# Attention of a two-layer graph network: two visits of eight heads in place of four visits of four

## The chip, the cores and the metric

The kernel runs on one core of one Trainium2 chip. The metric is device time in microseconds (us). Engines are named as in the profile: PE (TensorE matmuls), PEld (its weight loads), DVE (VectorE), ACT (ScalarE), POOL (GpSimd), SP (SyncE, which issues the DMAs here). All data are float32.

## The reference, cut to what matters

64 graphs of 256 nodes with 512 features pass two layers. Layer 0 is masked attention with eight heads of width 64, layer 1 a graph attention with one score per node.

```python
# layer 0
h = maximum(layernorm(x), 0)
q, k, v = h @ Wq + bq, h @ Wk + bk, h @ Wv + bv          # 8 heads of 64
attn = softmax(q @ k.T / 8 + (1 - adj) * -1e9)            # per head, 256 x 256
x = x + (attn @ v) @ Wo + bo
# layer 1
h = maximum(layernorm(x), 0); g = h @ W
e = leaky_relu(g @ a1 [:, None] + g @ a2 [None, :]) * adj
x = x + elu(softmax(e) @ g + beta * g)
```

## The kernel before, in words

**Work and order.** Graphs are taken in pairs, p = 0 to 31; pair p holds graphs g0 = 2p and g1 = 2p + 1. The order of every instruction on PE, DVE, ACT and POOL is the order in which the Python code issues it (a manual schedule), so what stands first in the code stands first in its engine's queue. A round of the steady part is `first_half(p)` and then `second_half(p)`; each round works on four pairs at once: q, k and v of pair p+1, attention of graphs around pair p, the output projection (`UnitO`) and layer norm of pair p-1, and layer 1 (`UnitW`) of pair p-2. `start`, `first`, `last` and `end` are the same work at the two ends.

**Units.** Every weight product of a pair is done as seven smaller products (a fast two-by-two block scheme). `Unit.p(i)` (L274) issues product i: four PE instructions of 128x256, which the trace shows as eight, since a float32 matmul is two passes. `products(u, 2, 7, 5)` (L635) issues several, with DVE's and ACT's additions behind them: product 6 has an addition at L285, product 7 one at L288, product 5 is followed by `put2`, product 3 by `put12`, product 2 by `put11`. Products 1 and 2 add up in one PSUM bank, 5 and 3 in another.

**Attention visits.** `scores(b, q)` (L413) computes the scores of four of a graph's eight heads (q is 0 or 1): 8 PE instructions with 64 rows each, two heads side by side in the array. ACT takes the exponential of each head into a `pt` tile (L424), POOL multiplies it by the mask (L425) and adds its two halves into `pp` (L427) for the row sums. `values(b, q)` (L442) multiplies the four `pt` tiles with v (L438, tiles of 32 columns, four heads side by side), sums the `pp` tiles with a matmul against ones (L447), and DVE takes the reciprocal (L449), adds the sums to a range check `acc` (L450) and scales the result into `oT` (L452). `acc` also takes the reciprocals, on POOL (L453), as a function that the next `scores` calls after its second head. A visit is `values` of one group of four heads and `scores` of a later one, back to back on PE; a round has four visits.

**PSUM.** There are eight banks under one tag. A visit takes one for the products with v, one for the sums and four for the scores; a unit takes five.

**Layer 1 scores.** After the output projection, `y_stats_0` to `y_stats_2` (L658 to L666, instructions at L248), `y_scales` (bn_aggr on DVE, then three small POOL instructions, L258 to L260) and `y_normal` (ACT, L507) give the normalised rows `h2` of pair p-1. `y_sums` (L513) is one DVE instruction per node tile and column: `pr = h2 * war` with a running sum into `s12`; a graph needs four. `gat_scores` (L516) transposes these sums with two PE instructions (`pe`, L171) and forms the scores `e` on DVE (L523 twice, L525); `gat_exp` is on ACT (L530); `gat_divide` is three DVE instructions per graph (L535, L537 twice), reading `e` and the constant `betai`; `gat_t` transposes `e` with four PE instructions (`at`, L546); `gat_z` (L559) multiplies it with `h2`.

**Where these stood.** In `second_half`, `y_sums` of graph g1-2 stood behind product 6 of the first q/k unit, `gat_scores` of both graphs of the pair in the second q/k unit, `divide` behind its product 7, and `gat_t` at the start of the v unit.

**Buffers.** `BUFS` gives buffers by tag: 4 for `pt`, 4 for `pp`, 8 for `y`, and separate tags for x (`xt`) and `h2`.

Of the kernel before, what the change touches and what calls it, by code (L numbers as in the profile page):

```python
# [16 lines left out]
P = 128  # L17
# [6 lines left out]
def kernel(ctx: ExitStack, tc: tile.TileContext, x, adj, wq, bq, wk, bk, wv, bv, wo, bo, w, a, beta, out):  # L24
# [33 lines left out]
    BUFS = {"set": 13, "qk": 8, "v": 4, "pt": 4, "xt": 4, "y": 8, "h2": 4, "e": 2, "eT": 2, "m": 2, "c": 3, "u": 4}  # L58
# [17 lines left out]
    def load(p, *which):  # L76
        for g in [2 * p + gi for gi in which or (0, 1)]:
            for t in range(NT):
                XT[g, t] = sb([P, D], "xt", f"x_{g}_{t}", BUFS["xt"])
                nc.sync.dma_start(XT[g, t], x[g, t * P:(t + 1) * P, :])  # L80
# [213 lines left out]
    def combine_31(s, a21, a22, tag="set"):  # L294

        s["tag"] = tag
        s[7] = blk(tag, f"s3_{s['name']}")
        a21(s[7], ALU.subtract, s[1])
        s[5] = blk(tag, f"s1_{s['name']}")
        a22(s[5], ALU.add, s["a21"])  # L300
# [112 lines left out]
    def scores(b, q, between=None):  # L413
        pss = [bank(f"sc_{b}_{q}_{i}") for i in range(4)]
        for pair in range(2):
            qk = QK.pop((b, 2 * q + pair))
            for k in range(NT):
                for h in range(2):
                    hs = slice(h * HD, (h + 1) * HD)
                    nc.tensor.matmul(pss[2 * pair + h][:, k * N:(k + 1) * N], qk[hs, 1, k * P:(k + 1) * P],  # L420
                                     qk[hs, 0, :], start=True, stop=True)
        for i in range(4):
            pt = PT[b, q, i] = blk("pt", f"pt_{b}_{q}_{i}")
            nc.scalar.activation(pt, two(pss[i]), AF.Exp, scale=QSCALE)  # L424
            nc.gpsimd.tensor_tensor(pt, pt, maskT, ALU.mult)  # L425
            pp = PP[b, q, i] = sb([P, N], "pp", f"pp_{b}_{q}_{i}", 4)
            nc.gpsimd.tensor_tensor(pp, pt[:, 0, :], pt[:, 1, :], ALU.add)  # L427
            if between and i in between:
                between[i]()
# [12 lines left out]
    def values(b, q):  # L442

        ps = weigh(V.pop((b, q)), [PT.pop((b, q, i)) for i in range(4)], f"{b}_{q}")
        sums = bank(f"sm_{b}_{q}")
        for i in range(4):
            nc.tensor.matmul(sums[i * HH:(i + 1) * HH, :N], ones[:, :HH], PP.pop((b, q, i)), start=True, stop=True)  # L447
        rec = sb([P, N], "rec", f"rec_{b}_{q}")
        nc.vector.reciprocal(rec, sums[:, :N])  # L449
        nc.vector.tensor_tensor(acc, sums[:, :N], acc, ALU.add)  # L450
        OT[b, q] = blk("set", f"oT_{b}_{q}")
        nc.vector.tensor_tensor(OT[b, q], two(ps), rec.unsqueeze(1).to_broadcast([P, 2, N]), ALU.mult)  # L452
        return lambda: nc.gpsimd.tensor_tensor(acc, acc, rec, ALU.add)  # L453
# [48 lines left out]
    def normal(g, rstd, nmr, tag="h2"):  # L502
        h2 = H2[g] = [sb([P, D], tag, f"h2_{g}_{t}", BUFS[tag]) for t in range(NT)]
        SC[g] = sb([P, NT, 2], "s12", f"s12_{g}", 3)
        for t in range(NT):
            for f in range(2):
                nc.scalar.activation(h2[t][:, f * N:(f + 1) * N], Y[g, f][:, t, :], AF.Relu, bias=nmr[:, t:t + 1],  # L507
                                     scale=rstd[:, t:t + 1])
# [68 lines left out]
    class UnitW(Unit):  # L577

        def __init__(self, p, tags=("m", "c")):
            self.pair, self.o, self.tags = p, {}, tags  # L580
            super().__init__(f"w_{p}", nodes_mm(A.pop(("z", p)), WW))

        def elu(self, gi, fh, src, o=None, step=None):
            g = 2 * self.pair + gi
            if not step:
                m = blk(self.tags[0] if (gi, fh) != (0, 0) else "m", f"m_{g}_{fh}")
                nc.scalar.activation(m, src, AF.Relu, scale=-1.0)
                nc.scalar.activation(m, m, AF.Exp, scale=-1.0)  # L588
                self.o[gi, fh] = (o or blk(self.tags[1], f"o_{g}_{fh}"), m)
            if step is not False:  # L590
                nc.vector.scalar_tensor_tensor(self.o[gi, fh][0], src, 0.0, Y.pop((g, fh)), op0=ALU.max, op1=ALU.add)

        def finish(self, gi, fh, eng):
            g = 2 * self.pair + gi
            o, m = self.o[gi, fh]
# [10 lines left out]
        def put2_sums(self):  # L606
            self.c = blk(self.tags[1], f"o_{2 * self.pair + 1}_1")
# [77 lines left out]
    def residuals(p, tag="y"):  # L685
        for gi, fh in ((0, 0), (1, 1), (1, 0), (0, 1)):
# [27 lines left out]
    def start():  # L714
# [42 lines left out]
        scores(0, 0)  # L757
        shift(0)
        products(uv, 4, 6)
        shift(1)  # L760
        products(uv, 2, 7, 5)
        shift(2)
        products(uv, 3)
        return wo_blocks

    def first():
        add = values(0, 0)
        scores(0, 1, {1: add})
        x_t(1)
        load(2)  # L770
        s = A["h", 1]
        ua, ub, uv = UnitQK(1, 0), UnitQK(1, 1), UnitV(1)
        ua.p(1)
        combine_24(s)
        products(ua, 4, 6)
        prods = project_a()
        prods(0)
        products(ua, 2, 7)
        add = values(0, 1)
        scores(1, 0, {1: add})  # L780
        residuals(0)
        products(ua, 5)
        ub.p(1)
        prods(1)
        products(ub, 4)
        products(ua, 3)
        products(ub, 6)
        prods(2)
        products(ub, 2)
        add = values(1, 0)  # L790
        scores(1, 1, {1: add})
        products(ub, 7, 5)
        uv.p(1)
        products(ub, 3)
        prods(3)
        prods(4)
        products(uv, 4)
        for i in range(2 * NT):
            x_stats(2, i)
        add = values(1, 1)  # L800
        x_scales(2)
        scores(2, 0, {1: add})
        o_blocks(0)
        products(uv, 6, 2)
        x_normals(2, *range(2 * NT))
        products(uv, 7, 5)
        prods(5)
        products(uv, 3)
        combine_24(A["o", 0])
        uo = UnitO(0)  # L810
        uo.p(1)
        uo.p(4)
        add = values(2, 0)
        scores(2, 1, {1: add})
        products(uo, 6, 2)
        return uo


    def first_half(p):
        g0, g1 = 2 * p, 2 * p + 1  # L820
        uw = UnitW(p - 2)
        uw.p(1)
        x_stats(p + 1, 0)
        x_stats(p + 1, 1)
        uw.p(4)
        x_stats(p + 1, 2)
        x_stats(p + 1, 3)
        products(uw, 6, 2, 7, 5)
# [3 lines left out]
        add = values(g0, 0)  # L832
        scores(g0, 1, {1: add})
# [3 lines left out]
        uo = UnitO(p - 1)  # L837
        uo.p(1)
# [8 lines left out]
        products(uo, 2)  # L847
        return uo

    def second_half(p, uo):  # L850
        g0, g1 = 2 * p, 2 * p + 1
        products(uo, 7)
        y_stats_0(p - 1)
        products(uo, 5)
        x_t(p + 1)
        if p + 2 < NP:
            load(p + 2)
        products(uo, 3)
        combine_2(A["h", p + 1])
        add = values(g0, 1)  # L860
        y_stats_1(p - 1)
        y_stats_2(p - 1)
        combine_4(A["h", p + 1])
        scores(g1, 0, {1: lambda: (add(), y_scales(p - 1))})
        ua, ub = UnitQK(p + 1, 0), UnitQK(p + 1, 1)
        products(ua, 1, 4)
        y_normal(p - 1, 1)
        products(ua, 6)
        y_sums(p - 1, 1, 0, 1)
        products(ua, 2)  # L870
        y_normal(p - 1, 0)
        products(ua, 7, 5)
        y_sums(p - 1, 0, 0)
        add = values(g1, 0)
        scores(g1, 1, {1: add})
        products(ua, 3)
        y_sums(p - 1, 0, 1)
        products(ub, 1, 4, 6)
        gat_scores(g1 - 2)
        products(ub, 2)  # L880
        gat_exp(g1 - 2)
        gat_scores(g0 - 2)
        gat_exp(g0 - 2)
        products(ub, 7)
        divide(p - 1)
        products(ub, 5)
        add = values(g1, 1)
        scores(g1 + 1, 0, {1: add})
        if p == NP - 2:
            o_blocks(p, "xt")  # L890
        residuals(p)
        uv = UnitV(p + 1)
        uv.p(1)
        gat_t(g1 - 2)
        gat_t(g0 - 2)
        products(ub, 3)
        products(uv, 4, 6, 2, 7, 5)
        if p == NP - 2:
            return uv
        gat_z(p - 1)  # L900
        products(uv, 3)
        combine_24(A["z", p - 1])

    def last(uv):
        p = NP - 1
        g0, g1 = 2 * p, 2 * p + 1
        combine_24(A["o", p - 1])
        add = values(g0, 0)
        scores(g0, 1, {1: add})
        products(uv, 3)  # L910
# [3 lines left out]
        add = values(g0, 1)  # L914
        scores(g1, 0, {1: add})
        products(uo, 5)
        y_stats_1(p - 1)
        gat_z(p - 2)
# [3 lines left out]
        combine_24(A["z", p - 2])  # L922
        add = values(g1, 0)
        scores(g1, 1, {0: lambda: y_normal(p - 1, 1), 1: add})
        uw = UnitW(p - 2, ("pt", "xt"))
        products(uw, 1, 4)
        y_sums(p - 1, 1, 0, 1)
        products(uw, 6)
        y_normal(p - 1, 0)
        products(uw, 2, 7)  # L930
        uw.finish(0, 0, nc.gpsimd)
        residual(p, 0, 0, "qk")
# [4 lines left out]
        add = values(g1, 1)  # L937
        o_blocks(p)
        residual(p, 1, 1, "qk")
        residual(p, 1, 0, "qk")  # L940
        residual(p, 0, 1, "qk")
        add()
        uw.put2_elu(False)
        uw.p(3)
        uo = UnitO(p)
        uo.p(1)
        uo.p(4)
        y_sums(p - 1, 0, 0)
        combine_24(A["o", p])
        y_sums(p - 1, 0, 1)  # L950
        return uw, uo

    def end(uw, uo):
        p = NP - 1
        g0, g1 = 2 * p, 2 * p + 1
        products(uo, 2)
        gat_scores(g0 - 2)
        gat_exp(g0 - 2)
        uo.p(6)
# [13 lines left out]
        normal(g1, rstd, minus(mr, f"y{g1}"), "qk")  # L973
# [6 lines left out]
        normal(g0, rstd, minus(mr, f"y{g0}"), "qk")  # L980
# [6 lines left out]
        uw = UnitW(p - 1, ("pt", "xt"))  # L987
# [16 lines left out]
        uw.put2_elu()  # L1004
        uw.p(3)
        gat_t(g0)
        uw.put12()
# [9 lines left out]
        uw = UnitW(p, ("pt", "xt"))  # L1017
# [16 lines left out]
    with tc.manual_schedule(engines={ENG.PE, ENG.DVE, ENG.Activation, ENG.Pool}):  # L1034
        WO = start()
        WW = {}
        uo = first()
        second_half(1, uo)
        for p in range(2, NP - 1):
            uv = second_half(p, first_half(p))  # L1040
        end(*last(uv))
# [16 lines left out]
    def general(src, dst, W, mask):  # L1058
        xt = sb([P, NT, D], "x", "fx", 1)
# [145 lines left out]
```

## Time and profile before

| what | value |
|---|---|
| median of 3 runs | 2856.28 us (2855.66 to 2856.35) |
| the profiled execution | 2857.51 us, span 2855.7 us |
| granted PE clock, mean | 0.997 |
| a round of the steady part (one `second_half` to the next in the timeline) | 88.09 us |
| recip L449 | 128 instructions, 1745 ns each |
| DVE `acc<-sm,acc` L450 | 128, 359 ns each |
| POOL `acc<-acc,rec` L453 | 128, 852 ns each |
| DVE `pr<-h,war` L513 | 256, 1228 ns each |
| POOL mask L425 / half sums L427 | 512 each, 1404 / 845 ns |

The span is from the first to the last instruction; the time of an execution has some 2 us more around it. In a timeline, a line is a group of like instructions that follow each other, with the start, the time, the engine, the line of the code and the tiles. PE's matmuls are pipelined and their ends modelled, so that the distance from one start to the next tells more than the time shown.

### The profile page before, as it was taken

The page shows a single profiled execution, that of the slowest core. Times are in us where ns is not written, and L with a number is a line of the kernel's source. Part 1 is how long each engine was busy: PE and PEld are TensorE (multiplying, and loading weights), DVE is VectorE, ACT ScalarE, POOL GpSimd, SP SyncE. Part 2 cuts the span into 40 slices and gives each one's busy share as a digit, 9 for nine tenths or more (in the row PEclk, how much of TensorE's full clock was granted, in tenths as well). Part 3 has the DMA queues.
Part 4 walks back from the last instruction along what each step waited for, and adds up shares of the span by engine and source line. Part 5 has one row for each costly group of instructions (what it writes and reads, how often), then busy time and mean ns, then how long its engine had stood idle before and what let it go on. Part 6 is the DMA issues. An engine that isn't in the chain of part 4 may idle for free. (4 is left out here: it accounts for less than half of the span.)

```text
span 2855.7 us, 46364 instructions
## 1 busy us (share of the span) xinstructions
PE 2837.8 (99%) x18110; PEld 2331.3 (82%) x18110; DVE 2067.1 (72%) x3651; ACT 1045.4 (37%) x2116; POOL 1624.5 (57%) x1592
## 2 busy tenths in 40 slices
PE   9999999999999999999999999999999999999997
PEld 8888888888888888888888888888888888888876
DVE  6776786767867677767777676786767877677767
ACT  3333433333433334333333333343333433334333
POOL 3755655556555556555575555655556655556572
PEclk9999999999999999999999999999999999999998
DMA  5000111100111001110011110111100111001001
GB/s 155 23 31 22 38 45 45 45 15 32 45 45 45 19 27 45 45 45 28 18 45 45 45 33 20 38 45 45 45 16 30 45 45 45 21 25 45 30 20 42
DMA packets 96479, 110.00 MB, mean 39 GB/s; under 512 B 8576, under 2 KB 79488, under 8 KB 96256
## 3 DMA queue, kind: packets, MB, share of 16 engines
q1 hardware_dynamic: 96256, 106.99, 12.0%
q8 instruction: 145, 2.38, 0.4%
q14 instruction: 78, 0.64, 0.1%
HBM read 73.41 MB, written 33.55 MB: 37 GB/s over the span
## 5 line engine op out<-in xcount | busy, mean ns | idle before, releaser
L425 POOL TENSOR_TENSOR pt<-pt,maskT 128x512 f32<-128x512 f32 x512 | 719.0, 1404 | 552.8 <-ACT pt L424 552.8
L427 POOL TENSOR_TENSOR pp<-pt 128x256 f32<-128x256 f32 x512 | 432.9, 845 | 40.2
L424 ACT ACTIVATE pt<-sc 128x512 f32<-128x512 f32 x512 | 264.4, 603 | 338.2 <-PE sc L420 332.0
L513 DVE SCALAR_TENSOR_TENSOR pr<-h,war 128x512 f32<-128x512 f32 x256 | 303.4, 1228 | 57.0 <-ACT h L507 57.0
L596 POOL TENSOR_TENSOR o<-o,m 128x512 f32<-128x512 f32 x40 | 50.6, 1268 | 515.1 <-ACT m L588 463.4
L420 PE MATMUL sc<-qk 64*128 64x256 f32 x2048 | 255.7, 389 | 0.0
L438 PE MATMUL av<-pt,v 128*32 128x256 f32 x4096 | 247.6, 382 | 0.0
L420 PEld LDWEIGHTS sc<-qk 64*128 64x128 f32 x2048 | 187.3, 186 | 69.7 <-PE av L438 38.3
L559 PE MATMUL pz<-eT,h 128*128 128x256 f32 x1024 | 226.8, 379 | 1.3 <-ACT eT L547 1.3
L449 DVE RECIPROCAL rec<-sm 128x256 f32<-128x256 f32 x128 | 223.3, 1745 | 3.5 <-PE sm L447 3.5
L559 PEld LDWEIGHTS pz<-eT,h 128*128 128x128 f32 x1024 | 194.9, 190 | 28.2 <-ACT eT L547 1.6
L438 PEld LDWEIGHTS av<-pt,v 128*32 128x32 f32 x4096 | 120.0, 109 | 108.4 <-issue 31.5
L356 PE MATMUL qk_p<-s_h,wq_t 128*128 128x256 f32 x768 | 197.4, 379 | 0.0
L356 PE MATMUL qk_p<-s_h,wk_t 128*128 128x256 f32 x768 | 197.1, 379 | 0.0
L389 PE MATMUL o_p<-wo_t,s_o 128*128 128x256 f32 x768 | 178.8, 383 | 0.2 <-ACT pt L424 0.2
L389 PE MATMUL w_p<-w_t,s_z 128*128 128x256 f32 x768 | 176.4, 379 | 0.3 <-DVE s_z L304 0.3
L389 PE MATMUL v_p<-wv_t,s_h 128*128 128x256 f32 x768 | 176.3, 379 | 0.0
L389 PEld LDWEIGHTS o_p<-wo_t,s_o 128*128 128x128 f32 x768 | 147.5, 192 | 21.3 <-ACT pt L424 0.9
L562 ACT COPY z<-pz 128x512 f32<-128x512 f32 x128 | 74.8, 586 | 244.2 <-PE pz L559 244.2
L573 DVE TENSOR_TENSOR s_z<-pz,z 128x512 f32<-128x512 f32 x64 | 44.1, 691 | 163.5 <-ACT z L562 163.5
L389 PEld LDWEIGHTS v_p<-wv_t,s_h 128*128 128x128 f32 x768 | 145.8, 190 | 20.1 <-ACT pt L424 0.3
L389 PEld LDWEIGHTS w_p<-w_t,s_z 128*128 128x128 f32 x768 | 145.6, 190 | 20.3 <-issue 0.6
(171 smaller groups left out, 5718.8 us busy)
## 6 DMA issues: line engine op xcount, KB each, us to landing
x<-in_x_dram SPq DMA_DIRECT2D x128, 256.0 KB, 3.6
y<-in_x_dram SPq DMA_DIRECT2D x128, 256.0 KB, 2.9
out_dram<-o SPq DMA_DIRECT2D x127, 256.0 KB, 2.2
wq_b<-in_L_gnn_Wq_dram SPq DMA_DIRECT2D x4, 256.0 KB, 5.4
wk_b<-in_L_gnn_Wk_dram SPq DMA_DIRECT2D x4, 256.0 KB, 5.6
wv_b<-in_L_gnn_Wv_dram SPq DMA_DIRECT2D x4, 256.0 KB, 4.9
wo_b<-in_L_gnn_Wo_dram SPq DMA_DIRECT2D x16, 64.0 KB, 3.3
w_b<-in_L_gnn_W_dram SPq DMA_DIRECT2D x4, 256.0 KB, 3.4
```

Source lines behind the costliest of these rows:

```text
L356: nc.tensor.matmul(ps[:, j * N:(j + 1) * N], wj[i][:, c, ft * P:(ft + 1) * P], s[i][:, c, :], start=(start and j == 0 and c == 0), stop=(c ...
L389: nc.tensor.matmul(ps[:, t * N:(t + 1) * N], s[i][:, c, t * P:(t + 1) * P], wj[i][:, c, :], start=(start and t == 0 and c == 0), stop=(c = ...
L420: nc.tensor.matmul(pss[2 * pair + h][:, k * N:(k + 1) * N], qk[hs, 1, k * P:(k + 1) * P], qk[hs, 0, :], start=True, stop=True)
L424: nc.scalar.activation(pt, two(pss[i]), AF.Exp, scale=QSCALE)
L425: nc.gpsimd.tensor_tensor(pt, pt, maskT, ALU.mult)
L427: nc.gpsimd.tensor_tensor(pp, pt[:, 0, :], pt[:, 1, :], ALU.add)
L438: nc.tensor.matmul(ps[i * HH:(i + 1) * HH, s * N:(s + 1) * N], v[:, k, c0:c0 + HH], pts[i][:, k, :], start=(k == 0), stop=(k == NT - 1))
L449: nc.vector.reciprocal(rec, sums[:, :N])
L513: nc.vector.scalar_tensor_tensor(pr, H2[g][t], 1.0, war[:, j, :], op0=ALU.mult, op1=ALU.mult, accum_out=SC[g][:, t, j:j + 1])
L559: nc.tensor.matmul(ps[:, f * N:(f + 1) * N], h2[k][:, fs], eT[:, k, :], start=(k == 0), stop=(k == NT - 1))
L562: nc.scalar.copy(dst, two(ps))
L596: eng.tensor_tensor(o, o, m, ALU.add)
```

## The change

It puts two `scores` calls into one and two `values` calls into one: `scores(b)` does the eight heads of a graph, `values(b)` the eight heads of a graph. A round has two visits: `values(g0)` with `scores(g1)`, and `values(g1)` with `scores(g1 + 1)`, both in `second_half`. `pt` and `pp` have eight buffers each.

`acc` takes the reciprocals on DVE, directly behind the scaling into `oT`. On DVE the built program has 128 instructions more than before, on POOL 128 fewer, and on PE as many as before.

Around it the rest of the round is put in a new order. `first_half` begins with `v_chain`: the v unit of the pair with, between its products, `gat_scores` and `gat_exp` of graph 2p-4, then `divide` of both graphs and their transposes. In `second_half`, `y_sums` of graph g1-2 stands behind product 5 of the first q/k unit and its additions, `gat_scores` of that graph behind product 4 of the second q/k unit; `y_sums` of g0-2 stands behind products 6 and 5 of the second. `project_a` (the products of W with the two score vectors) moves from `first` into `start`. x and `h2` share one tag of four buffers, `y` has six, the blocks of a second combination are written in place, and in `last` and `end` the layer 1 output is written in place of `y`. `last` and `end` have a new order too.

```diff
-    BUFS = {"set": 13, "qk": 8, "v": 4, "pt": 4, "xt": 4, "y": 8, "h2": 4, "e": 2, "eT": 2, "m": 2, "c": 3, "u": 4}
+    BUFS = {"set": 13, "qk": 8, "v": 4, "pt": 8, "x": 4, "y": 6, "e": 2, "eT": 2, "m": 2, "c": 3, "u": 4}
...
-    def scores(b, q, between=None):
+    def scores(b, between={}):
+        for q in range(2):
             pss = [bank(f"sc_{b}_{q}_{i}") for i in range(4)]
...
-                pp = PP[b, q, i] = sb([P, N], "pp", f"pp_{b}_{q}_{i}", 4)
+                pp = PP[b, q, i] = sb([P, N], "pp", f"pp_{b}_{q}_{i}", 8)
...
-    def values(b, q):
+    def values(b):
+        for q in range(2):
...
             nc.vector.tensor_tensor(OT[b, q], two(ps), rec.unsqueeze(1).to_broadcast([P, 2, N]), ALU.mult)
-        return lambda: nc.gpsimd.tensor_tensor(acc, acc, rec, ALU.add)
+            nc.vector.tensor_tensor(acc, acc, rec, ALU.add)
...
     def first_half(p):
+        uv = v_chain(p)
+        gat_z(p - 2)
+        load(p + 1)
+        residuals(p - 1, ((0, 0), (1, 1)))
+        products(uv, 3)
+        combine_24(A["z", p - 2])
         uw = UnitW(p - 2)
...
         uw.finish(0, 0, nc.gpsimd)
         o_blocks(p - 1)
         x_scales(p + 1)
-        add = values(g0, 0)
-        scores(g0, 1, {1: add})
+        residuals(p - 1, ((1, 0), (0, 1)))
+        uo = UnitO(p - 1)
+        uo.p(1)
         uw.p(3)
...
     def second_half(p, uo):
...
         products(uo, 3)
-        combine_2(A["h", p + 1])
-        add = values(g0, 1)
+        values(g0)
+        combine_24(A["h", p + 1])
         y_stats_1(p - 1)
         y_stats_2(p - 1)
-        combine_4(A["h", p + 1])
-        scores(g1, 0, {1: lambda: (add(), y_scales(p - 1))})
+        scores(g1, {(0, 2): lambda: y_scales(p - 1)})
         ua, ub = UnitQK(p + 1, 0), UnitQK(p + 1, 1)
-        products(ua, 1, 4)
+        products(ua, 1, 4, 6)
         y_normal(p - 1, 1)
-        products(ua, 6)
-        y_sums(p - 1, 1, 0, 1)
         products(ua, 2)
         y_normal(p - 1, 0)
         products(ua, 7, 5)
+        y_sums(p - 1, 1, 0, 1)
+        ub.p(1)
+        products(ua, 3)
+        ub.p(4)
+        gat_scores(g1 - 2)
+        gat_exp(g1 - 2)
+        ub.p(6)
         y_sums(p - 1, 0, 0)
-        add = values(g1, 0)
-        scores(g1, 1, {1: add})
-        products(ua, 3)
+        products(ub, 7, 5)
         y_sums(p - 1, 0, 1)
-        products(ub, 1, 4, 6)
-        gat_scores(g1 - 2)
-        products(ub, 2)
-        gat_exp(g1 - 2)
-        gat_scores(g0 - 2)
-        gat_exp(g0 - 2)
-        products(ub, 7)
-        divide(p - 1)
-        products(ub, 5)
-        add = values(g1, 1)
-        scores(g1 + 1, 0, {1: add})
...
+        products(ub, 2, 3)
+        values(g1)
+        scores(g1 + 1)
+
+    def v_chain(p):
+        uv = UnitV(p)
+        uv.p(1)
+        gat_scores(2 * p - 4)
+        gat_exp(2 * p - 4)
+        uv.p(4)
+        divide(p - 2)
+        products(uv, 6, 2)
+        gat_t(2 * p - 3)
+        gat_t(2 * p - 4)
+        products(uv, 7, 5)
+        return uv
...
     def last():
...
+        values(g1)
+        y_normal(p - 1, 1)
+        y_normal(p - 1, 0)
...
+        products(uw, 6)
         y_sums(p - 1, 1, 0, 1)
         products(uw, 2, 7)
         uw.finish(0, 0, nc.gpsimd)
         gat_scores(g1 - 2)
...
     def end(uw, uo):
...
         products(uo, 2)
+        uo.p(6)
         gat_scores(g0 - 2)
         gat_exp(g0 - 2)
-        uo.p(6)
```

## The prediction, made before the change was run

> **What bounds the kernel now.** I read the page's busy table first.
>
> ```profile
> span 2855.7 us, 46364 instructions
> ## 1 busy us (share of the span) xinstructions
> PE 2837.8 (99%) x18110; PEld 2331.3 (82%) x18110; DVE 2067.1 (72%) x3651; ACT 1045.4 (37%) x2116; POOL 1624.5 (57%) x1592
> ```
>
> PE is never without work, so only two things count: the pace at which PE starts its matmuls, and whether it is made to wait. The waits of PE alone say that it hardly waits at all; the two largest, one each near the end, are the two kinds of wait that the change moves into every round:
>
> ```profile
> PE pe L171 <- DVE pr L513: 4.0, 1, 4.0
> PE at L546 <- DVE e L537: 1.6, 1, 1.6
> ```
>
> For the pace, the timeline of PE around one visit; columns are start, time, and the count at the end:
>
> ```profile
> 1007.42 1.89 PE L389 MATMUL o_p<-wo_b,s_o 128*128 128x256 f32 x8
> 1009.24 1.93 PE L438 MATMUL av<-pt,v 128*32 128x256 f32 x32
> 1010.99 0.61 PE L447 MATMUL sm<-pp,ones 128*32 128x256 f32 x8
> 1011.54 2.00 PE L420 MATMUL sc<-qk 64*128 64x256 f32 x16
> 1013.47 1.13 PE L356 MATMUL qk_p<-h,wq_b 128*128 128x256 f32 x4
> 1014.43 1.03 PE L356 MATMUL qk_p<-h,wk_b 128*128 128x256 f32 x4
> 1015.29 1.03 PE L356 MATMUL qk_p<-h,wq_t 128*128 128x256 f32 x4
> ```
>
> Four full-size matmuls take 1015.29 - 1014.43 = 0.865 us, 0.216 each; a unit product (eight) takes 1.73. At that pace, with four v-tiles or two score-tiles side by side, the visit would be 8 x 0.216 for av, 2 x 0.216 for sm, 8 x 0.216 for sc. What is over that is paid at the changes of tile shape: before av 1009.24 - (1007.42 + 1.73) = 0.09; in av 1.75 - 1.73 = 0.02; sm 0.55 - 0.43 = 0.12; sc 1.93 - 1.73 = 0.20; the first four of the next unit 0.96 - 0.865 = 0.10. Sum **0.53 us a visit**. It is the same in each round.
>
> **The change, part by part.**
>
> *Fewer visits.* Before there are 127 visits of values and scores, afterwards 63; 64 times three shape changes go: 64 x 0.53 = **-34 us**. The new neighbours (sm to av, four score heads to the next four) keep their shape. If each still paid its 0.12 and 0.20, 0.21 a visit or 13 us would be left; I take 34, as the matmuls inside one shape run at 0.216.
>
> *Bank turnover inside the visit.* T = 0 is the first av. av and sm of eight heads take 4.48, then 16 pairs of score matmuls; the next unit starts at 4.48 + 3.46 + 0.20, about 8.13. The scores need 8 banks and take again those of the first av and sm. DVE: reciprocal from about 2.5 (1.68 to the next start), acc 0.27, oT 0.60, acc with rec about 0.35, then the same again: first half free at 5.2 (needed at 6.3), second acc at 7.4 (needed at 8.13). Nothing lost; margin 0.7. The **acc addition moved to DVE** sits in that chain; the nearest rows are 0.36 (L450) and L227, printed below, at 0.41 to 1.49. I take 0.35, as POOL has no mask yet.
>
> *Node sums before the second layer's scores (place A).* Nine products lie between visit and pe: 8.13 + 1.83 + 8 x 1.73 = 23.8. The four pr stand on DVE behind product 5 (ends 18.6), its wake-up (0.2, as L490 at 1005.87 behind a product that ended at 1005.67) and four L374 (0.40 each): they start at 20.4. Alone a pr takes 0.61 (1025.54 to the next start, 1026.15): four end at 22.9, in time. But POOL works on the masks, and its rows show what that does:
>
> ```profile
> 1021.51 0.73 POOL L427 TENSOR_TENSOR pp<-pt 128x256 f32<-128x256 f32 x1
> ...
> 1022.20 1.72 POOL L425 TENSOR_TENSOR pt<-pt,maskT 128x512 f32<-128x512 f32 x1
> ...
> 1022.72 1.74 DVE L513 SCALAR_TENSOR_TENSOR pr<-h,war 128x512 f32<-128x512 f32 x1
> ...
> 1023.99 1.07 POOL L427 TENSOR_TENSOR pp<-pt 128x256 f32<-128x256 f32 x1
> ...
> 1024.39 1.22 DVE L513 SCALAR_TENSOR_TENSOR pr<-h,war 128x512 f32<-128x512 f32 x1
> ...
> 1025.54 0.68 DVE L513 SCALAR_TENSOR_TENSOR pr<-h,war 128x512 f32<-128x512 f32 x1
> ```
>
> The two engines take turns: each pr ends about 0.5 after a POOL instruction ended, each POOL instruction starts its own work when the pr has ended. A mask and a half sum with a pr behind each are 1.67 + 1.15 = 2.82. Before, POOL's masks of four heads (2.04 a head, undisturbed) were over after two or three pr. Now it has eight heads: from 6.4 on 8 x 2.04 = 16.3, y_scales 1.5, three turns given to DVE 1.3, so until about 25.5. All four pr meet it: 4.5 to 6.2 by the phase, 5.5 taken, end 25.9. **PE waits 2.0 us** (1.1 to 2.8) in each of 30 rounds: **+60**. Behind the waiting pe stands all the rest of PE's work, and nothing makes up for it.
>
> *Divide inside the v unit (place B).* pe is at 10.0, DVE's two L523 end at 11.3, then L525 and twice (L535, two L537). PE wants the second `at` at 8.13 + 1.83 + 0.22 + 3 x 1.73 + 0.44 + 0.11 = 15.9. With POOL idle, as in before (median 482 ns), this ends at 13.7. Now the masks of the second visit run until 24. The nearest row for a 128x256 instruction of two SBUF operands against POOL is
>
> ```profile
> L227 DVE SCALAR_TENSOR_TENSOR prod<-w_b,a x16: 412/766/1494, 69.0 to 96.8; 128x256 f32<-128x256 f32 x16
> ```
>
> (least, median, most): 0.41 alone, up to 1.49 behind a mask, and 2.28 for two in a row (77.35 to 79.63). L525 waits about 0.5 and ends at 12.4, two pairs 4.6, L535 and the phase 0.5: 17.5. **PE waits 1.6 us** (0.6 to 2.6), 30 times: **+48**.
>
> The Trainium skill speaks of this in "SBUF — State Buffer", section "SBUF: two separate sides": the port pair that VectorE and GpSimd share is an exclusive lock, and a VectorE instruction with two SBUF inputs against a GpSimd one that reads SBUF blocks in full. The pr rows agree (0.61 against 1.15 and 1.67). The L537 rows, taken with POOL idle, cannot show it; if the rule did not hold for them, place B would cost 0.
>
> *The clock.* Stretches around the two late waits; the second number is PE's busy time, the third from the end the granted clock:
>
> ```profile
> 2785.40:2788.80 3.40, 1.08 (x6) 0.65 (x4) 3.37 (x3) 0.00 (x0) 3.40 (x3) 1.00 0.00 0
> 2788.80:2795.60 6.80, 5.13 (x13) 4.14 (x14) 4.95 (x10) 0.91 (x4) 1.06 (x1) 0.50 0.00 0
> 2795.60:2799.00 3.40, 2.90 (x14) 2.22 (x12) 2.66 (x6) 1.23 (x2) 3.04 (x3) 1.00 0.22 77
> 2799.00:2802.40 3.40, 2.04 (x10) 1.22 (x11) 3.25 (x7) 0.95 (x2) 0.72 (x1) 1.00 0.43 154
> 2802.40:2805.80 3.40, 3.40 (x10) 2.69 (x9) 3.30 (x10) 0.22 (x1) 0.00 (x0) 0.51 0.00 0
> ```
>
> A stretch with 1.08 or 2.04 us busy is followed by half clock, one with 2.90 is not. A wait of 2 us leaves 1.4 in its stretch if it falls in one. Each halved stretch costs 1.7; of 60 waits between none and 40 may trigger it: 0 to 65, I take **+18**, ten.
>
> The page "TensorE: Matmul & The Clock Gate", section "Part 1: The HAM clock gate", says that it takes an idle window of about 3.4 us to halve the clock; by it these waits would cost nothing here. The second event above, with 2.04 busy, differs from it.
>
> *Start and end.* In `start`, project_a now adds 4 weight sums and 8 L227 between the v products, all against masks: about 5 and 9 us on DVE. By DVE's queue the last v addition ends near 65 where PE wants it at 61, and product 3 waits 2.4 earlier: **+7** (0 to 12). In `last` and `end` DVE bounds: from the reciprocals of the last-but-one group to `at` it has about 31 us, as before; the late waits move from one pe to the other. I take 0 (-8 to +8).
>
> *Costs at nothing:* x and h2 in one tag: the loads of the next x wait for gat_z, 7 us ahead of their first use. The second combination (L304) ends 0.8 before product 6 of UnitO; if POOL held its operand longer, each round would pay the rest.
>
> Sum, against the profiled execution's 2857.5: -34 + 60 + 48 + 18 + 7 + 0 = +99, so 2956.5; the median of runs lies 1.2 lower: **2955 us**.
>
> **Rivals.**
>
> *No turn-taking where it hurts (faster).* If POOL is through with its masks at A and B, or DVE holds its place, both waits go: 2856.3 - 34 + 6 = **2828**. It decides once the two waits are under 34 / 30 = 1.1 us a round together. For it: four pr alone need 2.5 of the 3.4 us that they have. Against it: eight heads of masks last 16.3 us after the scores, and both places lie within them. Chance 0.15.
>
> *Only one place waits.* 2856.3 - 34 + 50 + 8 = **2880**: for it, the phase of POOL's instructions can favour B by 1 us. Chance 0.11.
>
> *The bank turnover stalls as well.* If DVE enters a visit 1.5 us late (output additions still queued), the second acc ends 0.8 after PE wants its bank: 63 x 0.8 = 50 on top, **3005** and more. For it, DVE's queue is full ahead of the first visit; against it, the margin of 0.7 above. Chance 0.08.
>
> *The change doesn't do what it says:* the shape changes stay; 13 in place of 34 saved, 2976, inside the forecast's own range.
>
> **How the numbers follow.** Forecast 0.66, its own range 2885 to 3010 (all low ends together give 2866, all high ones 3069; they won't come together). The range 2835 to 3015 leaves out the first rival and half of the third. Within 0.2% is about what runs of this kernel can tell from no change: faster 0.17 (the first rival, a little of the second), same 0.02, slower 0.81.
>
> **What would show it.** Visits: 63 av-sm-av-sm-sc groups, each entered and left with one 0.53. A: PE waiting for pr L515 about 30 times, 2 us each; B: for e L539 at `at`, as often, with L539 near 1 us in place of 0.48. PEclk below 9 in the middle if the clock reacts. Wrong if PE's waits stay near 10 us in all.

## The result, and the profile after

The changed kernel takes **2925.91 us** (median of four runs, 2925.81 to 2926.86) against 2856.04 for the kernel before: a ratio of **1.0245, 95% interval 1.0228 to 1.0263**, 69.9 us slower. The profiled execution is 2926.01 us with a span of 2924.1.

The first line of the busy table of the changed kernel and its row of PE, then the row of the granted clock over the 40 slices:

```profile
span 2924.1 us, 46443 instructions
...
PE 2815.4 (96%) x18110; PEld 2344.7 (80%) x18110; DVE 2158.2 (74%) x3779; ACT 1035.7 (35%) x2116; POOL 1525.4 (52%) x1464
...
PEclk9999999999999999999999999999999999999999
```

PE has the same 18110 matmuls. Its busy time is 22 us *less* than before (2837.8), yet the span is 68.4 longer: PE has become a little cheaper and much more idle. The waits of PE in the changed kernel say where (total us, times, longest):

```profile
PE pe L171 <- DVE pr L515: 59.6, 32, 2.6
PE at L548 <- DVE e L539: 31.8, 31, 3.6
```

One late wait of each kind near the end has become about thirty of each, one a round. PE's timeline around one visit of the changed kernel:

```profile
523.48 1.93 PE L440 MATMUL av<-pt,v 128*32 128x256 f32 x32
525.23 0.61 PE L449 MATMUL sm<-pp,ones 128*32 128x256 f32 x8
525.66 1.91 PE L440 MATMUL av<-pt,v 128*32 128x256 f32 x32
527.39 0.61 PE L449 MATMUL sm<-pp,ones 128*32 128x256 f32 x8
527.93 3.72 PE L422 MATMUL sc<-qk 64*128 64x256 f32 x32
531.59 1.99 PE L389 MATMUL v_p<-wv_b,h 128*128 128x256 f32 x8
```

From the first av to the next unit it is 8.11 us without a stall; two visits of before take 2 x 4.223. With what is paid at the edges (0.09 ahead of the visit, 0.10 behind it) a pair of visits made into one saves 0.535 us.

**Place A** in one round, all engines, with other rows left out; PE's two transpositions start at 512.46 and 514.59:

```profile
511.25 1.06 POOL L429 TENSOR_TENSOR pp<-pt 128x256 f32<-128x256 f32 x1
511.65 1.21 DVE L515 SCALAR_TENSOR_TENSOR pr<-h,war 128x512 f32<-128x512 f32 x1
...
512.27 1.71 POOL L427 TENSOR_TENSOR pt<-pt,maskT 128x512 f32<-128x512 f32 x1
512.46 0.27 PE L171 MATMUL pe<-ident,s 128*128 128x128 f32 x1
...
512.79 1.74 DVE L515 SCALAR_TENSOR_TENSOR pr<-h,war 128x512 f32<-128x512 f32 x1
...
514.06 1.05 POOL L429 TENSOR_TENSOR pp<-pt 128x256 f32<-128x256 f32 x1
...
514.59 0.13 PEld L171 LDWEIGHTS pe<-ident,s 128*128 128x128 f32 x1 [2.21 <-DVE pr L515]
514.59 0.32 PE L171 MATMUL pe<-ident,s 128*128 128x128 f32 x1 [1.86 <-DVE pr L515]
```

Two of the four node sums are seen here, taking turns with GpSimd. The first transposition finds its sums ready, the second waits. Against the first av of this visit (488.71), the four sums start at T = 20.35, the fourth has its start at 24.08 and hands DVE on at 25.75.

**Place B** in the next unit; columns as before:

```profile
535.98 2.17 DVE L539 SCALAR_TENSOR_TENSOR e<-e,grec,betai 128x256 f32<-128x256 f32 x2
...
536.42 1.45 POOL L427 TENSOR_TENSOR pt<-pt,maskT 128x512 f32<-128x512 f32 x1
...
538.25 2.17 DVE L539 SCALAR_TENSOR_TENSOR e<-e,grec,betai 128x256 f32<-128x256 f32 x2
...
540.48 0.55 PE L548 MATMUL at<-ident,e 128*128 128x128 f32 x3 [0.95 <-DVE e L539]
```

A pair of divisions takes 2.17 against the masks. In the kernel before, with GpSimd idle, a pair took 0.88, one alone 0.48 at the median:

```profile
1041.50 0.88 DVE L537 SCALAR_TENSOR_TENSOR e<-e,grec,betai 128x256 f32<-128x256 f32 x2
```

The even graph's e is ready at T = 16.9 of this visit (523.48).

**The account of the 68.4 us.** Gaps between matmul starts, read over the whole trace and sorted by what follows them: 64 pairs of visits x 0.535 = -34.2; place A +61.5 (30 waits of 2.05); place B +34.8 (30 of 1.16); start +4.7; the last pair and the end +2.0, half clock included; together 68.8. One round is 90.26 us after and 88.09 before; -2 x 0.535 + 2.05 + 1.16 = 2.14 explains the difference of 2.17.

### The profile page after: what moved, and what is told of

Same layout as the page of the kernel before. It is cut to its first block, busy times and chain, and to the rows that moved or that the text cites. A ratio compares the mean times of both kernels' runs of the same rounds, so it can differ in the third digit from the quotient of the medians.

```text
span 2924.1 us, 46443 instructions
## 1 busy us (share of the span) xinstructions
PE 2815.4 (96%) x18110; PEld 2344.7 (80%) x18110; DVE 2158.2 (74%) x3779; ACT 1035.7 (35%) x2116; POOL 1525.4 (52%) x1464
## 4 chain that ended last, share of the span: by engine, by line
## 5 line engine op out<-in xcount | busy, mean ns | idle before, releaser
L515 DVE SCALAR_TENSOR_TENSOR pr<-h,war 128x512 f32<-128x512 f32 x256 | 253.7, 1035 | 0.0
L472 POOL TENSOR_TENSOR y<-y,bo 128x512 f32<-128x512 f32 x128 | 161.3, 1283 | 0.0
L374 DVE SCALAR_TENSOR_TENSOR qk<-qk_p,bq,qk_u 128x256 f32<-128x256 f32 x192 | 92.1, 480 | 80.1 <-PE qk_p L356 80.0
L532 ACT ACTIVATE e<-e 128x256 f32<-128x256 f32 x128 | 52.2, 409 | 250.6 <-DVE e L527 250.6
L539 DVE SCALAR_TENSOR_TENSOR e<-e,grec,betai 128x256 f32<-128x256 f32 x128 | 134.2, 1087 | 2.3
L356 PE MATMUL qk_p<-h,wq_b 128*128 128x256 f32 x512 | 134.7, 386 | 0.3 <-ACT h L333 0.2
L596 DVE SCALAR_TENSOR_TENSOR o<-w_p,y 128x512 f32<-128x512 f32 x87 | 60.2, 692 | 99.7 <-ACT m L590 99.7
L509 ACT ACTIVATE h<-y,nmr_y,rstd_y 128x256 f32<-128x256 f32 x256 | 132.5, 591 | 1.1
L356 PE MATMUL qk_p<-h,wk_t 128*128 128x256 f32 x512 | 131.5, 379 | 0.0
L356 PE MATMUL qk_p<-s_h,wq_t 128*128 128x256 f32 x512 | 131.5, 379 | 0.0
```

What stands on the lines that cost most here:

```text
L356: nc.tensor.matmul(ps[:, j * N:(j + 1) * N], wj[i][:, c, ft * P:(ft + 1) * P], s[i][:, c, :], start=(start and j == 0 and c == 0), stop=(c ...
L472: nc.gpsimd.tensor_tensor(r, r, bo2[:, fh * N:(fh + 1) * N].unsqueeze(1).to_broadcast([P, 2, N]), ALU.add)
L515: nc.vector.scalar_tensor_tensor(pr, H2[g][t], 1.0, war[:, j, :], op0=ALU.mult, op1=ALU.mult, accum_out=SC[g][:, t, j:j + 1])
L539: nc.vector.scalar_tensor_tensor(e[:, t, :], e[:, t, :], rec[:, t:t + 1], betai[:, (1 - t) * P:(3 - t) * P], op0=ALU.mult, op1=ALU.add)
```

## Experiments

**1. Only place A undone.**

```diff
-        ub.p(4)
+        products(ub, 4, 6, 7, 5)
         gat_scores(g1 - 2)
         gat_exp(g1 - 2)
-        ub.p(6)
-        y_sums(p - 1, 0, 0)
-        products(ub, 7, 5)
-        y_sums(p - 1, 0, 1)
+        y_sums(p - 1, 0, 0, 1)
         products(ub, 2, 3)
```

> The second layer's scores of the odd graph are put two more products and one later (behind product 5 of the second query-key unit), so that the transposes pe are wanted at T = 29.0 in place of 23.8 (T = 0 is the first av of the visit); the node sums that they need ended at T = 25.8 in the profile of the changed kernel. Theory (the wait is the lateness of the four node sums, and nothing else is late behind them): the 30 waits of PE for pr go, 30 x 2.07 = 62 us, 2864 us. Rival (DVE is full there, so that the wait comes back at the next thing that PE wants from DVE): less than 20 us of gain, 2906 or more, with new waits of PE for DVE in the same stretch of the round.

Measured 2864.85 us (2863.62 to 2866.25), ratio to before 1.0031 (1.0020 to 1.0042): 61 us back of the changed kernel's time, as the theory has it. Waits of PE in this run, the two largest:

```profile
PE at L548 <- DVE e L539: 32.0, 31, 3.6
PE pe L171 <- DVE pr L515: 4.5, 2, 2.6
```

The thirty waits for pr are gone, those for e are untouched, and no new one has come. DVE was not full; the node sums were late for their date alone.

**2. Only place B undone.**

```diff
-        gat_t(2 * p - 4)
-        products(uv, 7, 5)
+        products(uv, 7)
+        gat_t(2 * p - 4)
+        products(uv, 5)
```

> The transposes at of the even graph stand one product later in the v unit (behind product 7), wanted at T = 17.6 in place of 15.9; the divided e was done at T = 16.9 in the changed kernel. Theory: the 30 waits of PE for e go, 30 x 1.16 = 35 us, 2891 us. Rival (the wait moves into product 3 of the v unit or gat_z, because the DVE additions of product 6 and 7 stand behind the contended divide): 10 us or less of gain, 2916 or more.

Measured 2891.72 us (2890.72 to 2892.73), ratio 1.0125 (1.0110 to 1.0141): 34 us back. The wait for e falls to its one case near the end:

```profile
PE pe L171 <- DVE pr L515: 59.6, 32, 2.6
PE at L548 <- DVE e L539: 3.6, 1, 3.6
```

One product of 1.73 us covers a lateness of 1.16. The two places are independent: each run shows the other's wait unchanged.

**3. Both undone, the visits of eight heads kept.** The edits of 1 and 2 together.

> Both moves at once, visits of eight heads kept. Theory (two separate waits, and the visits save 0.535 us each): 2926 - 62 - 35 = 2829 us, that is 27 us faster than the kernel before; the saving of the visits then shows as itself, 64 x 0.535 = 34 less 7 of start and end. Rival (the visits of eight heads cost something else that the waits hid, such as bank turnover once PE is early): 2850 or more, with PE waiting for DVE at the scores or at the next unit's first product.

Measured **2830.94 us** (2829.77 to 2831.49), ratio to the kernel before **0.9913 (0.9899 to 0.9927)**. The first line and PE's row of this run, then its two largest waits of PE:

```profile
span 2828.3 us, 46473 instructions
...
PE 2803.8 (99%) x18110; PEld 2346.5 (83%) x18110; DVE 2146.0 (76%) x3779; ACT 1031.6 (36%) x2116; POOL 1516.0 (54%) x1464
```

```profile
PE pe L171 <- DVE pr L515: 4.3, 2, 2.6
PE at L548 <- DVE e L539: 3.6, 1, 3.6
```

PE is back at 99%, and one round is 87.02 us, 1.07 less than before: two merged pairs of 0.535, with nothing paid anywhere else in the round. So the larger visits are a gain by themselves. What the change lost lies in the dates of two small consumers.

**4. GpSimd's masks for half the heads left out.** This kernel leaves out the mask multiplication of the second four heads of each visit; DVE's and PE's orders are those of the changed kernel.

```diff
-                nc.gpsimd.tensor_tensor(pt, pt, maskT, ALU.mult)
+                if q == 0:
+                    nc.gpsimd.tensor_tensor(pt, pt, maskT, ALU.mult)
```

> The changed kernel, with the mask multiplication on GpSimd left out for the second four heads of every visit (their half sums stay); nothing on DVE changes. Theory (DVE and GpSimd take turns, so the node sums are slow because the masks of eight heads last until T = 25): GpSimd is through by about T = 19, the four pr run at 0.61 and end at T = 22.9, no wait for pr: 62 us gone; the divide meets masks only until T = 14.5 and half sums after it, its wait falls from 1.16 to between 0 and 0.6: 2926 - 62 - 25 = 2839, 2829 to 2850. Rival (the DVE queue is simply too long there, whoever else runs): pr stays near its 1.4 mean in that place, and the time stays above 2900.

Measured 2843.89 us, one run. The four node sums of a round in this kernel, DVE's timeline, and GpSimd's beside them:

```profile
495.91 0.99 DVE L516 SCALAR_TENSOR_TENSOR pr<-h,war 128x512 f32<-128x512 f32 x1
...
496.83 1.21 DVE L516 SCALAR_TENSOR_TENSOR pr<-h,war 128x512 f32<-128x512 f32 x1
...
497.97 0.68 DVE L516 SCALAR_TENSOR_TENSOR pr<-h,war 128x512 f32<-128x512 f32 x1
...
498.58 0.68 DVE L516 SCALAR_TENSOR_TENSOR pr<-h,war 128x512 f32<-128x512 f32 x1
```

```profile
493.57 3.92 POOL L430 TENSOR_TENSOR pp<-pt 128x256 f32<-128x256 f32 x5
```

The sums start at T = 20.35 again, so DVE's queue is the same. While the half sums run (to 497.5), pr takes 0.99 and 1.21; once GpSimd is idle it takes 0.68. The four end at T = 23.6, and the wait for pr is gone from the rounds. The one for e at `at` is halved, 15.5 us in all against 31.8. The same instructions in the same places are late or in time by what GpSimd does: this run names the cause, where runs 1 and 2 only name the place. GpSimd was through at T = 21.9 and not at the expected 19 (it stood 1.86 us for the mv_y of DVE, and gave turns to DVE's sums), which is why they end at 23.6 and not at 22.9.

**5 and 6. A longer wait, to see when the clock answers.** Small reciprocals ahead of the node sums of place A, four in one kernel and twelve in the other.

```diff
+        for _ in range(4):
+            dly = sb([P, 64], "dly", "dly", 1)
+            nc.vector.reciprocal(dly, war[:, 0, :64])
         y_sums(p - 1, 1, 0, 1)
```

> The changed kernel with four small reciprocals (128x64, some 0.4 us each) put on DVE ahead of the four node sums of the odd graph, so that PE's wait in place A grows from 2.0 to about 3.5 us; this is to see when the clock answers. By the prediction's reading (a stretch of 3.40 us with about 2 us busy is followed by half clock, 1.7 us for each) half of the 30 waits or more are followed by matmuls at 0.43: 2926 + 45 + 25 or more = 2996 or more. Rival (only a stretch without any work of nearly its whole length halves the clock): a wait of 3.5 us seldom fills one, five or fewer of 30 are followed by half clock: 2971 to 2980.

> The same with twelve small reciprocals: the wait in place A grows to some 4.6 us or more. Both readings have half clock behind most of the 30 waits, if a wait is all that it takes: 2926 + 30 x 2.6 + 30 x 1.7 = 3055. If none of them is halved, the clock does not answer to waits of this length in mid-run at all: 3004.

Measured 3019.78 and 3085.08 us, one run each. The waits came out longer than designed: PE idles 4.1 to 4.2 us in a round with four, 6.1 with twelve. With four, 21 of 30 waits are followed by matmuls that start 0.427 apart, so the rival with five or fewer fell; with twelve, all 30 are. PE's timeline of the run with twelve:

```profile
539.32 0.29 PE L171 MATMUL pe<-ident,s 128*128 128x128 f32 x1 [4.75 <-DVE pr L515]
540.46 0.48 PE L171 MATMUL pe<-ident,s 128*128 128x128 f32 x1 [0.84 <-DVE pr L515]
540.73 1.92 PE L356 MATMUL qk_p<-s_h,wq_t 128*128 128x256 f32 x4
542.43 1.50 PE L356 MATMUL qk_p<-s_h,wk_t 128*128 128x256 f32 x4
543.77 1.03 PE L356 MATMUL qk_p<-s_h,wq_t 128*128 128x256 f32 x4
```

Four matmuls take 1.92 in the first row of qk_p and 1.03 in the last. Half clock costs 31 us in the kernel with four (147 starts, one more wait near the end among them, 0.213 too late each) and 38 in the rounds of the other (180 starts). So the clock does answer in mid-run, here to waits of twice the length that the change makes; what decides is worked out below.

**7. The node sums ahead of the unit's additions.**

```diff
+        y_sums(p - 1, 1, 0, 1)
         products(ua, 7, 5)
-        y_sums(p - 1, 1, 0, 1)
```

> The changed kernel with the node sums of the odd graph ahead of products 7 and 5 of the first query-key unit in place of behind them, and so ahead of that unit's additions on DVE. Theory (whatever stands on DVE against the masks is 5.5 us late, so the lateness goes to the additions): the sums run from about T = 18.3 to 24, the addition of product 7 and the four of product 5 follow, the first of them ends at T = 25, where PE wants the bank of product 3 at T = 20.4: PE waits 4 to 5 us there and no longer for pr, 2926 + 30 x 2.5 = 3000 us (2970 to 3020), more if the clock answers. Rival (only the place of the node sums behind the additions makes them late): the wait for pr goes and nothing takes its place, 2864.

Measured 3083.92 us (3083.57 to 3085.77), ratio 1.0796 (1.0777 to 1.0814). PE's largest wait, and DVE's last sum with what stands behind it:

```profile
PE qk_p L356 <- DVE qk L374: 148.0, 30, 5.0
```

```profile
532.85 1.74 DVE L515 SCALAR_TENSOR_TENSOR pr<-h,war 128x512 f32<-128x512 f32 x1
...
534.52 0.68 DVE L288 TENSOR_TENSOR qk_u<-qk_p,qk_u 128x512 f32<-128x512 f32 x1
535.31 0.48 DVE L374 SCALAR_TENSOR_TENSOR qk<-qk_p,bq,qk_u 128x256 f32<-128x256 f32 x1
```

The mechanism is that of the theory, with the first addition behind product 5 over at T = 25.0. The size is not: a wait of 5.1 us a round brings half clock behind every one of the 30, 57 us that the 3000 did not hold. Node sums behind the additions are the better order of the two; the dates of their consumer had to move with them.

**8. A version with the ends tended too.** Runs 1 and 2 together, and edits in `start`, `first`, `last` and `end`, in this order:

```diff
...
         products(uv, 2)
-        prods(0)
         products(uv, 7, 5)
-        prods(1)
...
-        products(ua, 1, 4, 6, 2, 7, 5)
+        products(ua, 1, 4)
+        prods(0)
+        products(ua, 6, 2, 7, 5)
...
+        products(ub, 4, 6, 7, 5, 2)
+        prods(1)
+        products(ub, 3)
...
-        gat_scores(g1 - 2)
-        gat_exp(g1 - 2)
         uw.p(5)
         uw.put2_sums()
         uo = UnitO(p)
         uo.p(1)
+        uo.p(4)
+        gat_scores(g1 - 2)
+        gat_exp(g1 - 2)
...
-        uo.p(4)
...
         uw.put2_elu(True)
+        divide(p - 1)
         uw.put12()
...
         products(uo, 7)
-        divide(p - 1)
```

> Both places relieved as in the run of both moves (2831), and three moves more, at the start and the end: the weight products of project_a out of the v unit of the start into places of the first visits where DVE is idle; in the last pair, the odd graph's scores behind two products more; in the end, the divide ahead of the last additions of the output unit. Theory (the stretches at both ends are plain lateness of DVE as well): 3.3 us at the start, 3.5 to 4.8 at the last pe, 1.7 to 2.9 at the last at, and up to 3 of half clock behind them: 2817 to 2824 us. Rival (the end is bound by DVE's whole queue, so that a moved wait comes back a few products later): 2828 to 2831.

Measured **2823.51 us** (2823.42 to 2824.23), ratio to the kernel before **0.9885 (0.9869 to 0.9902)**, the fastest here. The start gains its 3.3 us whole. At the end the rival has a part: the waits of 4.3 us for pr are gone and that of 3.6 for e is down to 2.3, but 1.4 us come back at a product w_p behind one addition and 2.5 at an o_p behind another. Moving one consumer there uncovers the next.

**9 and 10. What counts as work for the clock.** The kernel with twelve reciprocals, with PE given something to do in its wait: 46 transposes in one, 23 products in the other, none of whose results is used.

```diff
+            for i in range(46):
+                nc.tensor.transpose(ps[:, (2 + i % 2) * P:(3 + i % 2) * P], ident, ident)
         along(ps, [sc[:, t, 1:2] for t in range(NT)])
```

> The run with twelve reciprocals (place A: PE idle for some 6.1 us, half clock behind each of the 30), with 46 transposes of the identity, 0.109 each, put on PE ahead of the late pe, so that PE works for 5.0 of those 6.1 us on nothing that is used. Theory (the clock answers to stretches without matrix products, transposes do not count): half clock follows all 30 again, 3085 us less nothing, 3080 to 3090. Rival (the clock answers to idle time alone, and transposes are work): no half clock in the rounds, 40 us less, some 3048.

> The same with 23 products (128x256, 0.216 each, 5.0 us too) in place of the 46 transposes. Both readings have no half clock in the rounds, some 3045 us. If half clock follows nevertheless, neither reading is right.

Measured 3044.03 and 3161.33 us, one run each. PE's timeline in the run with transposes:

```profile
529.80 5.19 PE L524 MATMUL pe<-ident 128*128 128x128 f32 x46
534.82 0.27 PE L171 MATMUL pe<-ident,s 128*128 128x128 f32 x1
535.85 0.32 PE L171 MATMUL pe<-ident,s 128*128 128x128 f32 x1 [0.76 <-DVE pr L515]
536.01 1.03 PE L356 MATMUL qk_p<-s_h,wq_t 128*128 128x256 f32 x4
```

Full clock at once, in all 30 rounds: the theory fell, and the rival's 3048 is near. Transposes are work to the clock, and the 30 waits filled with transposes that nobody uses cost 41 us less than the same waits left empty. The run with products has no half clock in the rounds either; its time is longer since each such product is two matmuls in the trace (46 a round, 9.9 us), so it fills more than the wait. That was my mistake in designing it.

**11. The second addition into acc back on GpSimd**, on top of run 3: `values` leaves it to be issued behind the half sum of the next visit's second head.

> Both places relieved (2831), and the second addition into acc given back to GpSimd, behind the half sum of a visit's second head, as before the change. Theory (that addition, 0.4 to 1.3 us on DVE, is off the path in either place as long as the two waits are gone): 2831, 2828 to 2834. Rival 1 (on DVE it stands in the turnover of the banks and costs PE something): faster by more than 5 us. Rival 2 (GpSimd's masks move 1.4 us back and the divide and the node sums with them): slower by 10 or more, with waits for e at the transposes at.

Measured 2831.48 us (2829.63 to 2833.23), ratio 0.9914 (0.9898 to 0.9931), against 2830.94 for run 3: no difference. Which engine adds it does not matter once the two places have room.

## The prediction, step by step

**Right on mechanism and sign; 2955 forecast, 2925.91 measured, inside the range of 2835 to 3015.** By its own terms, in us of the profiled execution:

| step | predicted | measured |
|---|---|---|
| fewer visits | -34 | -34.2 |
| bank turnover | 0 | 0 |
| place A | +60 | +61.5 |
| place B | +48 | +34.8 |
| clock | +18 | 0 in the rounds |
| start | +7 | +4.7 |
| end | 0 | +2.0 |
| sum | +99 | +68.8 (span: +68.4) |

*Fewer visits* held to the second digit; the new neighbours inside a visit pay nothing, so the rival in which the change does not do what it says is out. Run 3 shows the saving by itself.

*Bank turnover:* no loss, and the second acc is done at T = 7.42 as worked out (7.4), but the margin was mis-read. The next unit's first weight load is at T = 8.11. What the trace names as its releaser is the second oT, done at T = 8.02, in the visit at 523.48, and the second acc, there done only at T = 8.03, in the visit at 488.71. Neither was late: the load's idle time of 0.33 us is the same as in the kernel before (at 1013.46), and both visits take 8.11. Room was about 0.1, not 0.7; it just sufficed.

*Place A:* start 20.35 (predicted 20.4), end 25.8 (25.9), wait 2.05 (2.0). Run 4 shows the turn-taking as its cause, runs 1 and 3 that nothing else stood behind it. The rule of the Trainium skill ("SBUF — State Buffer", section "SBUF: two separate sides") agrees in kind: pr takes 0.68 with GpSimd idle and 0.99 to 1.75 against it, with DVE's queue the same.

*Place B* was mis-sized. L527 ended at 12.4 as predicted and a pair takes 2.27, predicted 2.3. What failed is the 0.5 added for "L535 and the phase": the second pair follows the first at once, the small reciprocal inside the turn, and e is ready at 16.9, not 17.5. The wait is 1.16 in place of 1.6: 13 us of the 31 that the sum was over.

*The clock* is the step that failed: +18, from "a stretch with 1.08 or 2.04 us busy is followed by half clock". None of the 60 waits in the rounds is followed by half clock. Over the kernels run here, the idle time of PE between two products, and how often matmuls at 0.427 follow:

| PE idle, us | where | followed by half clock |
|---|---|---|
| 1.15 to 1.2 | place B, 7 kernels | 0 of 210 |
| 1.9 to 2.1 | place A, changed kernel and run 2 | 0 of 58 |
| 2.55 | first v unit of the start, 10 kernels | 5 of 10 |
| 2.84 | before, one wait near the end | 1 of 1 |
| 3.6 to 4.1 | runs 5 and 7 | 12 of 21 |
| 4.2 and more | before, runs 5 to 7, all ends | all of some 90 |

By the length of the wait alone, the limit lies between 2.1 and 2.55 us, and from there to 4.2 the same wait halves the clock in some cases and not in others. The granted clock shows why. In each of the thirteen profiles every change of it between full and half stands on a grid of 3.413 us (in run 5 the first three stretches of half clock begin at 58.6, 157.6 and 249.7, which is 29 and 27 steps apart), and what counts is how long PE works in one stretch of that grid. Stretches with PE's busy time and, third from the end, the granted clock, two pairs from run 5 and one from the changed kernel:

```profile
154.16:157.57 3.41, 1.32 (x7) 1.00 0.00 0
157.57:160.99 3.42, 3.42 (x10) 0.50 0.02 5
...
341.89:345.30 3.41, 1.43 (x7) 1.00 0.00 0
345.30:348.72 3.42, 3.42 (x17) 1.00 0.00 0
```

```profile
602.02:605.43 3.41, 1.53 (x8) 1.00 0.02 5
605.43:608.84 3.41, 3.41 (x17) 1.00 0.00 0
```

Over the thirteen profiles, of the stretches at full clock (without the first four of each), all 123 with PE busy for 1.40 us or less are followed by half clock, and of 10,856 with 1.41 or more one is. That one is the event that the prediction read as 2.04 us busy: its stretch lies on the grid too, with 2.10 us busy, but behind its wait stand short matmuls with small gaps, 2.84 us of idle time in all, so that it was no measure for a single wait.

So the +18 came to nothing by a small margin, and that was luck: in eleven of the 30 rounds the wait of place A lay whole in one stretch, with 1.53 to 1.58 us busy. An estimate from these times and run 6: waits longer by some 0.2 us would have put these eleven over the limit, at 1.3 us each.

The Trainium skill ("TensorE: Matmul & The Clock Gate", section "Part 1: The HAM clock gate") says that the window of about 3.4 us runs freely and that an idle one halves the clock. The grid of 3.413 us agrees. For waits of 2.05 the skill was right (no cost) where my reading was wrong; that a window with 1.40 us of work in it still halves the clock, it does not say.

*Start and end:* the start's 4.7 holds 3.3 of waits for v's additions: product 3 waits 2.4 as predicted, the addition behind it costs 0.9 more, not 4. At the end the late pe and `at` have grown, a later wait has shrunk, and the end is 2.0 longer in all.

*The rivals:* both waits came, so neither "no turn-taking" nor "only one place waits" happened; the first one's 2828 is what run 3 measures (2831), once the waits are taken out by other means.

## What to carry to other kernels

When an edit groups work on one engine (eight heads of masks in a row), look for every small operation on the other engine that now falls into that stretch, and move its consumer by what it is late: two waits of 2.05 and 1.16 us a round cost 96 us and hid a true gain of 34, and moving two lines behind one to three more products got both back. Work a date out from the round's own rows, as T behind a fixed point, for the producer and for the consumer: here the dates of place A held to 0.1 us, and the terms that failed most were the ones added for caution (the clock's by luck). A short wait costs only itself; one that leaves PE no more than 1.4 us of work in a stretch of 3.41 costs the clock as well, and whether a wait of 2 to 4 us does so depends on where it falls in the grid.

## What the runs showed of the hardware

- The clock answers to how little PE works in a stretch of 3.41 us that the kernel does not set, and transposes whose results nobody uses count as work: 46 of them in a 6 us wait took the half clock away from 30 of 30 rounds (3085 to 3044 us).
- One half-clock episode cost 1.3 us in the rounds of run 6 (38 us for 30 waits of 6.1) and 1.9 in those of run 7 (57 for 30 of 5.1). The longer wait has the shorter episode: the granted clock is halved for one stretch of 3.41 us in 26 of the 30 rounds of run 6, and for two, 6.83 us, in every round of run 7.
- The slowdown between DVE and GpSimd can be seen instruction by instruction and both ways: a mask takes 1.27 alone and 1.71 with a node sum ahead of it, a half sum 0.73 and 1.06.
